# Layer 1's totals over channels and keys: 32x32 transpositions, VectorE sums and one small product each, in place of products with a matrix of ones

## The chip, the cores and the metric

The kernel runs on one core of one Trainium2 chip. The metric is the device time of one launch in microseconds. The core has five engines with instruction streams of their own: PE (TensorE, matrix products; its weight loads are listed apart as PEld), DVE (VectorE), ACT (ScalarE), POOL (GpSimd) and SP (SyncE, which here only issues DMAs). They wait for each other through semaphores. Everything is float32.

## The reference, cut to what matters

Two layers are computed on x of shape (8, 512, 32, 32), that is 8 images of C = 512 channels and N = 1024 positions. Layer 0 is an attention with group norms and 8 heads and is not touched by the change. Layer 1 is this, with one head of 512 channels:

```python
w_qkv = _weight_norm(v_qkv, g_qkv)
qkv = jnp.einsum('oc,bcn->bon', w_qkv, xt)
rms = jnp.sqrt(jnp.mean(jnp.square(qkv), axis=1, keepdims=True)) + 0.0001
qkv = qkv / rms
scores = jnp.einsum('bci,bcj->bij', q, k) * C ** (-0.5)
attn = jax.nn.softmax(scores, axis=-1)
h = jnp.einsum('bij,bcj->bci', attn, v)
h = jnp.einsum('oc,bcn->bon', w_out, h)
return (x + h) * 2.0 ** (-0.5)
```

Two totals over rows of a matrix matter here. The mean of squares (`rms`) needs, for each of the 1024 positions, a total over channels. The softmax needs, for each of the 1024 queries, a total of exponentials over the 1024 keys. In the kernel channels and keys both lie on the 128 partitions, so both totals run across partitions.

## The kernel before

One image is one *block* (`b`, 0 to 7); a block takes some 392 us. The program order on every engine is the order in which the Python code issues the instructions (`InOrder`, lines 26 to 34), so the order in the text is the order in each queue. A block has two parts.

**The heads of layer 0** (`Heads`, lines 534 to 628) run 32 steps: scores on PE, maxima and 32x32 transpositions on DVE, exponentials on ACT, scaling on POOL, and DMAs that regroup the transposed probabilities. Projections for the next block are woven in.

**Layer 0's end and layer 1.** `finish_layer0` (line 813) projects and normalises; then `Layer1.project` (line 895) does the following.

- Lines 900 to 908: four products with a Gram matrix (`py`), each multiplied with x on DVE and added to `acc`, a 128x1024 tile. Summed over partitions, `acc` is the square sum of each position. `acc` and `part` are the two halves of the tile `xy`.
- Lines 1014 to 1018: two `score_unit`s. Each is a `Seven` (lines 722 to 811): seven products `p_u`, of two matmuls with 512 columns each, where a plain product would take eight, drained by DVE and ACT into `u`. Inside the first unit, behind its third product (`(m, k) == (0, 2)`), `square_sums` (line 916) runs: eight products `ss`, with 128 columns of `acc` as the weights each, and two columns of ones. DVE turns `ss` into `rinv` = 1/rms with 14 small operations (`rsqrt` is three Newton steps). `broadcast` (line 925) writes `rinv` to DRAM (`far_rinv`, element by element, as the partition is the inner index there) and reads it back as a row on all partitions (`rrow`, in the place of `part`). POOL multiplies `u` by `rrow`.
- Lines 1023 to 1026: four `value_unit`s (`p_v`); ACT scales half of their results by `rinv`.
- Lines 1034 to 1037: four `weight_unit`s (`p_e`). ACT takes exponentials into `e`, and POOL adds them up into two 128x512 tiles `esum`, one for each half `th` of the queries (lines 1006 to 1009). In the last unit the half `th` = 1 is finished first.

Then the block's last loop (lines 1327 to 1340) runs the products `po` = v times e for `th` = 0, and the four groups of channels `c`, each of eight matmuls into one PSUM bank. `total(th)` (line 1042) multiplies `esum` with a matrix that is filled with the square root of 2 (`pe`, 512 columns; the result is the total, repeated on all partitions) and takes the reciprocal of it on DVE. `keep(th, c)` (line 1057) multiplies `po` by it and adds to x. The loads of x for block b + 2 (`load_x`, line 1325) are issued ahead of the loop; their statistics follow at `c` = 2 (lines 1331 to 1335), and the group norm's small products `pm` and `pv` at `norm_step`: `pm` in the middle of `c` = 3, `pv` in the middle of the product behind the loop (line 1343). Then the next block's heads start with `scores(0)` (line 1347). The products `th` = 1, `c` = 1 to 3 are done between the next heads' first steps (line 1348). For the last block they stand alone (lines 1356 to 1359).

PSUM comes from two pools. `ps_s` has three tiles of two banks (`wide`, tag `sc`), used in turn by the `Seven`s' products, `py`, `pe`, the norm's `pm` and `pv`, and the heads' scores. `ps_m` has two tiles of one bank (`bank`, tag `mm`). A tile can be taken anew only when all that read its predecessor in the same place are done.

Of the kernel before, what the change touches and what calls it, by code (L numbers as in the profile page):

```python
# [8 lines left out]
F32 = mybir.dt.float32  # L9
I32 = mybir.dt.int32  # L10
AF = mybir.ActivationFunctionType
ALU = mybir.AluOpType
AX = mybir.AxisListType
P = 128
# [38 lines left out]
def attention_blocks_kernel(  # L53
# [41 lines left out]
    pair = ctx.enter_context(tc.tile_pool(name="pair", bufs=2))  # L95
    prob = ctx.enter_context(tc.tile_pool(name="prob", bufs=2))
    block = ctx.enter_context(tc.tile_pool(name="block", bufs=2))
    sum_pool = ctx.enter_context(tc.tile_pool(name="sums", bufs=2))
    small = ctx.enter_context(tc.tile_pool(name="small", bufs=3))
    dram = ctx.enter_context(tc.tile_pool(name="dram", bufs=1, space=DRAM))  # L100
    ps_s = ctx.enter_context(tc.tile_pool(name="ps_s", bufs=3, space=PSUM))
    ps_m = ctx.enter_context(tc.tile_pool(name="ps_m", bufs=2, space=PSUM))
# [75 lines left out]
    for g in range(NG):  # L178
        VE.tensor_scalar(gavg[:, g, :], gavg[:, g, :], member[:, g : g + 1], None, ALU.mult)
    gavg = gavg.rearrange("p g s -> p (g s)")  # L180
    ones = const.tile([P, P], F32, name="ones")
    VE.memset(ones, 1.0)
    root2 = const.tile([P, P], F32, name="root2")
    VE.memset(root2, 2.0 ** 0.5)
    shift = const.tile([P, 1], F32, name="shift")
    VE.memset(shift, -16.0)
    cols = const.tile([P, NCOLS], F32, name="cols")
# [6 lines left out]

    def rsqrt_steps(r, v, n, name):

        t = small.tile([P, 4 * CI], F32, tag="rs_t", name=f"rs_{name}")[:, :n]
        VE.tensor_scalar(r.bitcast(I32), v.bitcast(I32), -0.5, 1597463007.0, ALU.mult, ALU.add)
        yield
        for _ in range(3):  # L200
            VE.scalar_tensor_tensor(t, r, -0.5, r, ALU.mult, ALU.mult)
            VE.tensor_mul(t, t, v)
            VE.scalar_tensor_tensor(r, t, 1.5, r, ALU.add, ALU.mult)
            yield
# [19 lines left out]
    far["qk0"] = dram.tile([P, 2, CI, P], F32, tag="far_qk0", name="far_qk0")  # L224
    far["qk7"] = dram.tile([P, 14, C - P], F32, tag="far_qk7", name="far_qk7")
    near = {}
    far_rinv = dram.tile([NT, P], F32, tag="far_rinv", name="far_rinv")

    def place(name, b):
        tag, shape = places[name]  # L230
# [87 lines left out]
    class Norm1:  # L318


        def __init__(self, b, xt, bank=bank):
            self.b, self.xt = b, xt
            self.st = small.tile([P, CI, 2, 6], F32, tag="gn_st1", name=f"st1_{b}")
            self.mv = small.tile([P, CI, 2], F32, tag="gn_mv1", name=f"mv1_{b}")
            self.gn = GroupNorm(self.mv, CI, G1S, G1B, f"1_{b}", bank)

# [327 lines left out]
    def finish_last(b, h, xt, o, begun):  # L654

        def project_out(j, th, pm):
            terms = out_terms(h.a, j, th, range(CI // 2, CI))
            if j in begun.pm:  # L660
                PE.matmul(pm[:, th, :], *terms[1], start=False, stop=True)
            else:
                run(matmuls(pm[:, th, :], terms))

        st = small.tile([P, CI, 2, 6], F32, tag="gn_st2", name=f"st2_{b}")
        mv = small.tile([P, CI, 2], F32, tag="gn_mv2", name=f"mv2_{b}")
        for j in range(CI):
            pm = begun.pm[j] if j in begun.pm else wide(f"pp_{b}_{j}")
            for th in range(2):
                project_out(j, th, pm)  # L670
            VE.tensor_add(o[:, j, :], o[:, j, :], pm.rearrange("p a f -> p (a f)"))
            for k in range(2):
                gn_stats(st[:, j], o[:, j, :], k)
            VE.bn_aggr(mv[:, j, :], st[:, j])
        fetch("gram", b)
        norm = GroupNorm(mv, CI, G2S, G2B, f"2_{b}")
        norm.means()
        a, c = norm.coeffs()
        for j in range(CI):
            AC.activation(o[:, j, :], o[:, j, :], AF.Identity, bias=c[:, j : j + 1], scale=a[:, j : j + 1])  # L680
            VE.tensor_add(xt[:, j, :], xt[:, j, :], o[:, j, :])
        slots.give(f"a_{b}")
        slots.give(f"o_{b}")
# [129 lines left out]
    def finish_layer0(b, h, rhs, xt, v0):  # L813

        o, w = big(f"o_{b}"), near["proj7"]
        st = small.tile([P, CI, 2, 6], F32, tag="gn_st2", name=f"st2_{b}")
        mv = small.tile([P, CI, 2], F32, tag="gn_mv2", name=f"mv2_{b}")
        norm = GroupNorm(mv, CI, G2S, G2B, f"2_{b}")

# [64 lines left out]
    class Layer1:  # L884
# [4 lines left out]
        def __init__(self, b, xt):  # L889
            self.b, self.xt = b, xt  # L890
            self.rhs = RightSide(xt, *(block.tile([P, 2, 2, HN], F32, tag="pb", name=f"t{k}_{b}") for k in (12, 34)))
            self.right = self.rhs.columns
            self.e, self.sums = {}, {}

        def project(self, hn_next):
            b, xt = self.b, self.xt
# [10 lines left out]
                if cj:  # L907
                    VE.tensor_add(acc, acc, part)

            ss = ps_m.tile([P, NT, 2], F32, tag="mm", name=f"ss_{b}")  # L910
            rinv = self.rinv = small.tile([P, NT], F32, tag="rinv", name=f"rinv_{b}")
            ms = small.tile([P, NT], F32, tag="ms", name=f"ms_{b}")
            rrow = part
            waiting = []

            def square_sums():
                for t in range(NT):
                    PE.matmul(ss[:, t, :], acc[:, t * P : (t + 1) * P], ones[:, :2], start=True, stop=True)
                VE.tensor_scalar(ms, ss[:, :, 0], 1.0 / (3 * C), 0.0, ALU.mult, ALU.max)
                rsqrt(rinv, ms, NT, f"r_{b}")  # L920
                VE.tensor_mul(rinv, rinv, ms)
                VE.tensor_scalar_add(rinv, rinv, 1e-4)
                VE.reciprocal(rinv, rinv)

            def broadcast():

                SY.dma_start(out=far_rinv.rearrange("t p -> p t"), in_=rinv)
                SY.dma_start(out=rrow, in_=far_rinv.rearrange("t p -> (t p)").partition_broadcast(P))
                for f in waiting:
                    f()  # L930
                waiting.clear()
                self.rrow = rrow
# [40 lines left out]
            def sum_u():  # L973

                s12 = prob.tile([P, 2, 2, HN], F32, tag="p", name=f"s12_{b}")
                s34 = prob.tile([P, 2, 2, HN], F32, tag="p", name=f"s34_{b}")
                q1, q2 = halves_
                self.s12, self.s34 = s12, s34
                for th in range(2):
                    e[th] = big(f"e_{b}_{th}", NT)  # L980
                    self.sums[th] = sum_pool.tile([P, HN], F32, tag="esum", name=f"esum_{b}_{th}")
                VE.tensor_add(s12[:, 0], u[:, :2, q2], u[:, 2:, q2])
                yield
                VE.tensor_sub(s12[:, 1], s12[:, 0], u[:, :2, q1])
                yield
                VE.tensor_sub(s34[:, 0], u[:, :2, q1], u[:, :2, q2])
                yield
                VE.tensor_sub(s34[:, 1], u[:, 2:, q1], s12[:, 1])

            def weight_unit(m):  # L990
# [9 lines left out]

                def last(which):
                    th, t = int(which[0]) - 1, m + 4 * (int(which[1]) - 1)
                    et, esum = c[which], self.sums[th]
                    AC.activation(et, et, AF.Exp, bias=shift, scale=rinv[:, t : t + 1])
                    done[th].append(et)
                    if len(done[th]) == 2:
# [6 lines left out]
            done = ([], [])  # L1013
            for m in range(2):
                for k, _ in enumerate(score_unit(m).steps()):
                    if (m, k) == (0, 2):
                        square_sums()
                        broadcast()
            if b + 1 < B:
                for j in (1, 2):  # L1020
# [18 lines left out]
            Seven.half = None  # L1039
            slots.give(f"u_{b}")  # L1040

        def total(self, th):

            pe = ps_s.tile([P, HN], F32, tag="sc", name=f"pe_{self.b}_{th}")
            PE.matmul(pe, root2, self.sums[th], start=True, stop=True)
            VE.reciprocal(self.sums[th], pe)

        def products(self, th, c, between=None):
            self.po = bank(f"po1_{self.b}_{th}_{c}")
            e = self.e[th]  # L1050

            terms = [(self.v[:, t, c * P : (c + 1) * P], e[:, t, :]) for t in (0, 4, 1, 5, 2, 6, 7, 3)]
            for k, _ in enumerate(matmuls(self.po, terms)):
                if k == 1 and between:
                    between()

        def keep(self, th, c):

            hs = slice(th * HN, (th + 1) * HN)

            share = near["v#"][:, N : N + HN] if self.b + 1 < B else self.po
            VE.tensor_mul(share, self.po, self.sums[th])
            VE.scalar_tensor_tensor(self.xt[:, c, hs], self.xt[:, c, hs], 2.0 ** -0.5, share, ALU.mult, ALU.add)
            if th == 1:
                SY.dma_start(out=ov[self.b, :, c, :], in_=self.xt[:, c, :])
# [136 lines left out]
    for b in range(B):  # L1202
# [117 lines left out]
        if b + 2 < B:  # L1320

            hn_next = big(f"hn_{b + 2}")
            norm1 = Norm1(b + 2, hn_next, lambda name: wide(name)[:, 0])
            for c in range(CI):
                load_x(b + 2, hn_next, c)
            steps = norm1.gn.all_steps()
        for c in range(CI):
            one.products(0, c, norm_step if c == CI - 1 else None)
            if c == 0:
                one.total(0)  # L1330
            if c == 2 and b + 2 < B:
                for ci in range(CI):
                    for k in range(2):
                        norm1.stats(ci, k)
                norm1.aggregate()
            if c == CI - 1:
                norm_step()
            one.keep(0, c)
            if c == 1:
                one.total(1)  # L1340
        slots.give(f"e_{b}_0")
        if more:
            one.products(1, 0, norm_step)
# [49 lines left out]
```

## Time and profile before

| what | value |
|---|---|
| time, median of 3 runs | 3246.95 us (3246.25 to 3247.75) |
| the profiled execution's own time | 3249.17 us |
| its span in the trace | 3246.7 us |
| granted TensorE clock, mean | 0.998 of full speed |
| DVE busy | 2274.4 us, 70% |
| POOL busy | 1253.0 us, 39% |
| reciprocal of `pe`, 128x512 | 16 times, mean 3353 ns |
| `ss` matmuls in the records | 128 (two records for one float32 product), busy 14.7 us |
| `pe` matmuls in the records | 32, busy 16.3 us |
| write of `rinv` to DRAM, 4 KB | 10.7 us from issue to landing |
| read of it to all partitions, 512 KB | 5.2 us |

The span runs from the first to the last instruction in the trace. "Busy" is the time in which an engine has at least one instruction in work; ends of matmuls are modelled, so a busy PE need not be at its peak. The chain of waits is followed back from the last instruction: at each step to whatever released it, or to the instruction ahead of it on its engine.

### The profile page before, as it was taken

Reading aid. Unit: us, or ns where it says so; the run is one execution under the profiler, and the core shown is the slowest. Engines: PE = TensorE matmul, PEld = TensorE weight load, DVE = VectorE, ACT = ScalarE, POOL = GpSimd, SP = SyncE. Lnnn points to the kernel's source line nnn. Section 1 sums busy time; section 2 is a strip of 40 time slices with the busy share of each in tenths; the row PEclk is TensorE's granted clock in tenths of the full one; section 3 lists DMA queues with packets and bytes.
Section 4 is the critical chain, followed back from the end, with each engine's and each line's share of the span. In section 5 each row is a group of like instructions: output and inputs, shape, how many; then the busy total and the mean of one; then the engine's idle time right before and its main releaser. Section 6 shows DMA issues by size and latency. Waiting matters only on the chain.

```text
span 3246.7 us, 36723 instructions
## 1 busy us (share of the span) xinstructions
PE 3217.5 (99%) x13346; PEld 1657.8 (51%) x13346; DVE 2274.4 (70%) x3074; ACT 1045.7 (32%) x1813; POOL 1253.0 (39%) x1025
## 2 busy tenths in 40 slices
PE   8999999999999999999999999999999999999899
PEld 5445644455444554445544555445554456444454
DVE  5697667876678756886668866687667876578643
ACT  2453114521145211551215412254123531145210
POOL 1554224732257212671227603265223642246121
PEclk9999999999999999999999999999999999999999
DMA  6776215862168511784228822388214872158500
GB/s 201 213 203 209 75 49 155 219 193 59 49 183 229 171 43 56 202 229 138 52 77 214 229 96 63 95 219 242 78 49 115 216 214 75 23 157 210 183 7 26
DMA packets 231579, 447.34 MB, mean 138 GB/s; under 512 B 28996, under 2 KB 69480, under 8 KB 225512
## 3 DMA queue, kind: packets, MB, share of 16 engines
q1 hardware_dynamic: 231280, 444.97, 49.0%
q8 instruction: 107, 1.75, 0.2%
q14 instruction: 72, 0.59, 0.1%
q10 hardware_dynamic: 120, 0.02, 0.0%
HBM read 133.06 MB, written 29.52 MB: 50 GB/s over the span
## 4 chain that ended last, share of the span: by engine, by line
PE 93%; DMA 3%; DVE 2%; SPq 1%; issue 1%; POOL 0%; DVEq 0%
PE po L34 26%; PE s L34 13%; PE pq L34 7%; PE p_e_T L34 7%; PE p_v_T L34 6%; PE p_e_B L34 5%; PE p_v_B L34 5%; PE py L34 4%; PE pqk L34 4%; PE p_u_T L34 3%; PE p_o_T L34 3%; DMA pT<-pb 3%; PE p_u_B L34 3%; PE p_o_B L34 2%; SPq L34 1%; DVE pb L34 1%
## 5 line engine op out<-in xcount | busy, mean ns | idle before, releaser
L34 POOL TENSOR_SCALAR p<-p,tt 128x1024 f32<-128x1024 f32 x512 | 565.9, 1118 | 753.7 <-DVE tt L34 734.9
L34 ACT ACTIVATE p<-s,nm 128x1024 f32<-128x1024 f32 x512 | 565.7, 1109 | 887.7 <-DVE nm L34 794.1
L34 DVE TENSOR_REDUCE nm<-s 128x1 f32<-128x1024 f32 x512 | 602.0, 1217 | 158.9 <-PE s L34 158.6
L34 DVE STREAM_TRANSPOSE pb<-p 128x2048 f32<-128x2048 f32 x256 | 589.6, 2303 | 45.6 <-DMA pT<-pb 20.8
L34 PE MATMUL s<-qk 64*128 64x512 f32 x2048 | 526.5, 604 | 0.6
L34 PE MATMUL po<-pT,v 128*64 128x256 f32 x4096 | 471.7, 383 | 3.5 <-DMA pT<-pb 3.4
L34 PE MATMUL po<-e,v 128*128 128x512 f32 x1024 | 451.7, 595 | 0.0
L34 PEld LDWEIGHTS po<-pT,v 128*64 128x64 f32 x4096 | 285.9, 137 | 220.8 <-ACT v L34 32.6
L34 PEld LDWEIGHTS s<-qk 64*128 64x128 f32 x2048 | 199.5, 186 | 253.3 <-issue 227.9
L34 PEld LDWEIGHTS po<-e,v 128*128 128x128 f32 x1024 | 191.9, 190 | 245.0 <-issue 236.4
L34 POOL TENSOR_TENSOR u<-u,xy 128x512 f32<-128x512 f32 x64 | 78.9, 1270 | 335.4 <-DMA xy<-far_rinv 261.4
L34 PE MATMUL pq<-hn,qk 64*128 64x512 f32 x504 | 197.1, 592 | 0.0
L34 POOL TENSOR_TENSOR esum<-esum,e 128x512 f32<-128x512 f32 x96 | 130.5, 1360 | 154.2 <-ACT e L34 151.7
L34 POOL TENSOR_TENSOR x<-x,o 128x1024 f32<-128x1024 f32 x21 | 52.1, 2512 | 348.3 <-ACT o L34 348.3
L34 ACT ACTIVATE e<-e,shift,rinv 128x512 f32<-128x512 f32 x128 | 100.9, 812 | 256.6 <-DVE e L34 256.6
L34 DVE TENSOR_TENSOR e<-e,p_e_T 128x512 f32<-128x512 f32 x160 | 106.9, 684 | 86.5 <-PE p_e_T L34 84.3
L34 DVE TENSOR_TENSOR v<-v,p_v_T 128x256 f32<-128x256 f32 x300 | 114.2, 415 | 68.7 <-PE p_v_T L34 50.0
L34 PE MATMUL pqk<-hn,qk 64*128 64x512 f32 (+1 forms) x672 | 158.2, 590 | 0.0
L34 PE MATMUL pq<-t,qk 64*128 64x512 f32 x336 | 150.9, 589 | 0.0
L34 PE MATMUL pq<-v,qk 64*128 64x512 f32 x336 | 150.9, 589 | 0.0
L34 PE MATMUL p_e_T<-s,t 128*128 128x512 f32 x320 | 147.8, 592 | 0.0
L34 PE MATMUL py<-x,gram 128*128 128x512 f32 x320 | 140.2, 597 | 5.4 <-issue 5.4
(215 smaller groups left out, 4130.9 us busy)
## 6 DMA issues: line engine op xcount, KB each, us to landing
pT<-pb SPq DMA_DIRECT2D x1024, 256.0 KB, 4.4
qk<-far_qk SPq DMA_DIRECT2D x21, 896.0 KB, 8.6
hn<-in_x_dram SPq DMA_DIRECT2D x32, 512.0 KB, 5.8
x<-in_x_dram SPq DMA_DIRECT2D x32, 512.0 KB, 4.5
out_dram<-x SPq DMA_DIRECT2D x32, 512.0 KB, 3.8
score<-far_score SPq DMA_DIRECT2D x8, 1792.0 KB
value<-far_value SPq DMA_DIRECT2D x8, 1792.0 KB, 7.2
proj<-far_proj SPq DMA_DIRECT2D x7, 1792.0 KB
```

Source lines behind the costliest of these rows:

```text
L34: return lambda *args, **kw: self._pin(call(*args, **kw))
```

## The change

All weights of the products with ones become a matrix `same` that holds 1 where two partitions have the same number modulo 32, and all data are folded by 32 first. `VE.transpose` turns each 32x32 square of a tile, and `tensor_reduce` adds up each 32 neighbouring columns; both together leave, from 128x1024, a tile of 128x32 in which partition 32 g + j and column B hold the sum over the 32 partitions of group g for position 32 B + j. One product with `same` adds the four groups g and leaves the total on each of the four. From there a 32x32 transposition gives 32 rows of 32 positions; `spread` writes them to DRAM as one row and reads that row to all partitions.

For the square sums this takes the place of eight products, and `rinv` is taken out of the 32-column form by four small copies. The small product moves behind the fourth product of the first score unit. For the exponentials it takes the place of two products of 512 columns and of two reciprocals of 128x512; one reciprocal of 128x32 and the way through DRAM come in. Both halves of `esum` are one tile now. In the last loop `po` lies two by two in `wide` tiles, `keep` runs for two groups of channels at once behind each second one, the loads of x are split in two (two ahead of the loop, two behind the spread), and so are the statistics. Some small tiles move to a pool with one buffer.

```diff
     block = ctx.enter_context(tc.tile_pool(name="block", bufs=2))
-    sum_pool = ctx.enter_context(tc.tile_pool(name="sums", bufs=2))
+    sum_pool = ctx.enter_context(tc.tile_pool(name="sums", bufs=1))
     small = ctx.enter_context(tc.tile_pool(name="small", bufs=3))
+    tiny = ctx.enter_context(tc.tile_pool(name="tiny", bufs=1))
     dram = ctx.enter_context(tc.tile_pool(name="dram", bufs=1, space=DRAM))
...
     gavg = gavg.rearrange("p g s -> p (g s)")
-    ones = const.tile([P, P], F32, name="ones")
-    VE.memset(ones, 1.0)
-    root2 = const.tile([P, P], F32, name="root2")
-    VE.memset(root2, 2.0 ** 0.5)
+    SQ = 32
+    same = const.tile([P, P], F32, name="same")
+    same2 = const.tile([P, P], F32, name="same2")
+    VE.tensor_reduce(flat := tiny.tile([P, SQ], F32, tag="flat", name="member32"), ident.rearrange("p (g i) -> p i g", i=SQ), AX.X, ALU.add)
+    for g in range(P // SQ):
+        VE.tensor_copy(same[:, g * SQ : (g + 1) * SQ], flat)
+    VE.tensor_scalar_mul(same2, same, 2.0 ** 0.5)
     shift = const.tile([P, 1], F32, name="shift")
...
-        t = small.tile([P, 4 * CI], F32, tag="rs_t", name=f"rs_{name}")[:, :n]
+        t = tiny.tile([P, SQ], F32, tag="rs_t", name=f"rs_{name}")[:, :n]
         VE.tensor_scalar(r.bitcast(I32), v.bitcast(I32), -0.5, 1597463007.0, ALU.mult, ALU.add)
...
     near = {}
-    far_rinv = dram.tile([NT, P], F32, tag="far_rinv", name="far_rinv")
+    far_rows = {k: dram.tile([SQ, SQ], F32, tag=f"far_{k}", name=f"far_{k}") for k in ("rinv", "esum")}
+    def square_sums(part, src, turned):
+        VE.transpose(turned, src)
+        VE.tensor_reduce(part, turned.rearrange("p (B j) -> p B j", j=SQ), AX.X, ALU.add)
+    def spread(row, vals, k, name):
+        flat = tiny.tile([P, SQ], F32, tag="flat", name=f"flat_{name}")
+        VE.transpose(flat, vals)
+        SY.dma_start(out=far_rows[k], in_=flat[:SQ])
+        SY.dma_start(out=row, in_=far_rows[k].rearrange("B i -> (B i)").partition_broadcast(P))
...
             self.b, self.xt = b, xt
-            self.st = small.tile([P, CI, 2, 6], F32, tag="gn_st1", name=f"st1_{b}")
+            self.st = tiny.tile([P, CI, 2, 6], F32, tag="gn_st1", name=f"st1_{b}")
             self.mv = small.tile([P, CI, 2], F32, tag="gn_mv1", name=f"mv1_{b}")
...
-        st = small.tile([P, CI, 2, 6], F32, tag="gn_st2", name=f"st2_{b}")
+        st = tiny.tile([P, CI, 2, 6], F32, tag="gn_st2", name=f"st2_{b}")
         mv = small.tile([P, CI, 2], F32, tag="gn_mv2", name=f"mv2_{b}")
...
         o, w = big(f"o_{b}"), near["proj7"]
-        st = small.tile([P, CI, 2, 6], F32, tag="gn_st2", name=f"st2_{b}")
+        st = tiny.tile([P, CI, 2, 6], F32, tag="gn_st2", name=f"st2_{b}")
         mv = small.tile([P, CI, 2], F32, tag="gn_mv2", name=f"mv2_{b}")
...
             self.right = self.rhs.columns
-            self.e, self.sums = {}, {}
+            self.e, self.sums, self.po = {}, None, {}
...
-            ss = ps_m.tile([P, NT, 2], F32, tag="mm", name=f"ss_{b}")
+            part_ss, r32, ms = (tiny.tile([P, SQ], F32, tag=t, name=f"{t}_{b}") for t in ("part", "r32", "ms"))
             rinv = self.rinv = small.tile([P, NT], F32, tag="rinv", name=f"rinv_{b}")
-            ms = small.tile([P, NT], F32, tag="ms", name=f"ms_{b}")
             rrow = part
             waiting = []
-            def square_sums():
-                for t in range(NT):
-                    PE.matmul(ss[:, t, :], acc[:, t * P : (t + 1) * P], ones[:, :2], start=True, stop=True)
-                VE.tensor_scalar(ms, ss[:, :, 0], 1.0 / (3 * C), 0.0, ALU.mult, ALU.max)
-                rsqrt(rinv, ms, NT, f"r_{b}")
-                VE.tensor_mul(rinv, rinv, ms)
-                VE.tensor_scalar_add(rinv, rinv, 1e-4)
-                VE.reciprocal(rinv, rinv)
+            square_sums(part_ss, acc, part)
+            def roots():
+                ss = bank(f"ss_{b}", SQ)
+                PE.matmul(ss, same, part_ss, start=True, stop=True)
+                VE.tensor_scalar(ms, ss, 1.0 / (3 * C), 0.0, ALU.mult, ALU.max)
+                rsqrt(r32, ms, SQ, f"r_{b}")
+                VE.tensor_mul(r32, r32, ms)
+                VE.tensor_scalar_add(r32, r32, 1e-4)
+                VE.reciprocal(r32, r32)
 ...
-                SY.dma_start(out=far_rinv.rearrange("t p -> p t"), in_=rinv)
-                SY.dma_start(out=rrow, in_=far_rinv.rearrange("t p -> (t p)").partition_broadcast(P))
+                spread(rrow, r32, "rinv", f"r_{b}")
+                for g in range(P // SQ):
+                    gs = slice(g * SQ, (g + 1) * SQ)
+                    VE.tensor_copy(rinv[gs], r32[gs].rearrange("p (t g) -> p g t", g=P // SQ)[:, g])
                 for f in waiting:
...
                 self.s12, self.s34 = s12, s34
+                self.sums = sum_pool.tile([P, N], F32, tag="esum", name=f"esum_{b}")
                 for th in range(2):
                     e[th] = big(f"e_{b}_{th}", NT)
-                    self.sums[th] = sum_pool.tile([P, HN], F32, tag="esum", name=f"esum_{b}_{th}")
                 VE.tensor_add(s12[:, 0], u[:, :2, q2], u[:, 2:, q2])
...
                     th, t = int(which[0]) - 1, m + 4 * (int(which[1]) - 1)
-                    et, esum = c[which], self.sums[th]
+                    et, esum = c[which], self.sums[:, halves_[th]]
                     AC.activation(et, et, AF.Exp, bias=shift, scale=rinv[:, t : t + 1])
...
                 for k, _ in enumerate(score_unit(m).steps()):
-                    if (m, k) == (0, 2):
-                        square_sums()
+                    if (m, k) == (0, 3):
+                        roots()
                         broadcast()
...
-        def total(self, th):
-            pe = ps_s.tile([P, HN], F32, tag="sc", name=f"pe_{self.b}_{th}")
-            PE.matmul(pe, root2, self.sums[th], start=True, stop=True)
-            VE.reciprocal(self.sums[th], pe)
-        def products(self, th, c, between=None):
-            self.po = bank(f"po1_{self.b}_{th}_{c}")
+        def square_sums(self):
+            self.part = tiny.tile([P, SQ], F32, tag="part", name=f"part_e_{self.b}")
+            turned = prob.tile([P, N], F32, tag="p", name=f"turned_{self.b}")
+            for th in (1, 0):
+                hs, n = slice(th * HN, (th + 1) * HN), SQ // 2
+                square_sums(self.part[:, th * n : (th + 1) * n], self.sums[:, hs], turned[:, hs])
+        def total(self):
+            pe = ps_s.tile([P, SQ], F32, tag="sc", name=f"pe_{self.b}")
+            PE.matmul(pe, same2, self.part, start=True, stop=True)
+            inv = tiny.tile([P, SQ], F32, tag="r32", name=f"inv_e_{self.b}")
+            VE.reciprocal(inv, pe)
+            spread(self.sums, inv, "esum", f"e_{self.b}")
+        def products(self, th, c, between=None, po=None):
+            po = self.po[th, c] = bank(f"po1_{self.b}_{th}_{c}") if po is None else po
             e = self.e[th]
 ...
             terms = [(self.v[:, t, c * P : (c + 1) * P], e[:, t, :]) for t in (0, 4, 1, 5, 2, 6, 7, 3)]
-            for k, _ in enumerate(matmuls(self.po, terms)):
+            for k, _ in enumerate(matmuls(po, terms)):
                 if k == 1 and between:
...
-            share = near["v#"][:, N : N + HN] if self.b + 1 < B else self.po
-            VE.tensor_mul(share, self.po, self.sums[th])
+            po = self.po.pop((th, c))
+            share = near["v#"][:, N : N + HN] if self.b + 1 < B else po
+            VE.tensor_mul(share, po, self.sums[:, hs])
             VE.scalar_tensor_tensor(self.xt[:, c, hs], self.xt[:, c, hs], 2.0 ** -0.5, share, ALU.mult, ALU.add)
...
             norm1 = Norm1(b + 2, hn_next, lambda name: wide(name)[:, 0])
-            for c in range(CI):
+            for c in range(2):
                 load_x(b + 2, hn_next, c)
             steps = norm1.gn.all_steps()
+        one.square_sums()
         for c in range(CI):
-            one.products(0, c, norm_step if c == CI - 1 else None)
+            if c % 2 == 0:
+                po = wide(f"po1_{b}_0_{c}")
+            one.products(0, c, norm_step if c == CI - 1 else None, po[:, c % 2])
             if c == 0:
-                one.total(0)
-            if c == 2 and b + 2 < B:
-                for ci in range(CI):
+                one.total()
+                if b + 2 < B:
+                    for ci in range(2, CI):
+                        load_x(b + 2, hn_next, ci)
+            if c and b + 2 < B:
+                for ci in range(CI)[2 * c - 2 : 2 * c]:
                     for k in range(2):
                         norm1.stats(ci, k)
-                norm1.aggregate()
+                if c == 2:
+                    norm1.aggregate()
             if c == CI - 1:
                 norm_step()
-            one.keep(0, c)
-            if c == 1:
-                one.total(1)
+            if c % 2:
+                one.keep(0, c - 1)
+                one.keep(0, c)
         slots.give(f"e_{b}_0")
```

## The prediction

> **What bounds the kernel now.** I read the page first: the line of busy times, and the shares of the chain of waits.
>
> ```profile
> PE 3217.5 (99%) x13346; PEld 1657.8 (51%) x13346; DVE 2274.4 (70%) x3074; ACT 1045.7 (32%) x1813; POOL 1253.0 (39%) x1025
> PE 93%; DMA 3%; DVE 2%; SPq 1%; issue 1%; POOL 0%; DVEq 0%
> ```
>
> PE is busy 99% of the span. A busy PE could still be one that waits with its modelled ends drawn out, so next come the waits of PE: over the whole run 23 us, nearly all in the first 10 us and in the last block, and only 3.4 us of it in the heads:
>
> ```profile
> PE po L34 <- DMA pT<-pb: 3.4, 3, 2.8
> ```
>
> Then the chain in order of time, for the first block (start, duration; x counts records, two for each float32 product). The other blocks have the same distances within 0.1 us.
>
> ```profile
> 355.92 3.43 PE p_u_B L34 x8
> 359.36 1.72 PE p_u_T L34 x4
> 361.07 1.68 PE ss L34 x16
> 362.75 5.26 PE p_u_T L34 x12
> ...
> 453.98 6.87 PE po L34 x16
> 460.85 0.86 PE pe L34 x2
> 461.71 6.87 PE po L34 x16
> 468.57 0.86 PE pe L34 x2
> 469.43 10.30 PE po L34 x24
> 479.73 0.12 PE pm L34 x2
> 479.85 6.97 PE po L34 x16
> 486.82 0.12 PE pv L34 x2
> 486.94 3.54 PE po L34 x8
> 490.48 1.92 PE s L34 x8
> ```
>
> Each piece starts where the one before it ends. So in layer 1 PE's own instructions are the path, and what is taken off PE there moves all that follows.
>
> **The sum on PE.** From 359.36 to 368.01 stand 16 `p_u` records (6.87 at their pace) and `ss`: `ss` costs 8.65 - 6.87 = 1.78 us. Two `pe` cost 469.43 - 453.98 - 2 x 6.87 = 1.71. Gone: 3.49 us a block. New: two products with 128 columns of weights and 32 moving columns. Their nearest row is `pm` and `pv` (4 columns, the same weights): from 469.43 to 490.48 stand three groups of `po` (20.61) and these two, so 0.22 each, 0.44 together. Saved: 3.05 us a block, times 8 = **24.4 us**. Bounds of a small product: 0.12 (its own piece in the chain) and 0.4 (two weight loads of 190 ns fully exposed), so 26.0 to 21.5 in all.
>
> One rule speaks against this sum. The Trainium skill, "TensorE: Matmul & The Clock Gate", section "Back-to-back issue gap", gives 1 to 64 moving columns some 60 cycles, 25 ns. By that the 16 `ss` records cost 0.4 us, and the change saves only 1.7 + 0.4 - 0.1 = 2.0 us a block, 16 in all. The row has 1.68 / 16 = 105 ns a record, because weights change each time; the same page's "LDWEIGHTS" (128 columns / 1.2 = 107 ns) fits it. I take the row.
>
> **Square sums: is the new product ready?** DVE finishes `acc` at 358.45 (the last `xy<-xy` starts at 357.22 and takes 1.23). Then comes a transposition of 1024 columns (estimate 1.17, half of the heads' 2303 ns for 2048 plus a little) and a reduction of 1024 (1217 ns by the heads' maxima): ready at about 361.0. PE is there behind the fourth `p_u` product, at 355.92 + 4 x 1.72 = 362.8. It doesn't wait; the cover is 1.8 us. Behind the 2.4 us on DVE stand the first unit's drains: `u<-u,p_u_B` at 360.01 moves to 361. Their PSUM tile is needed again by the seventh product at 366.4, so that is covered by 5 us. The 14 small operations are at 0.20 us spacing for 8 columns and some 0.23 for 32; with the transposition and four copies (0.15 to 0.2 each) DVE is through at about 367.5, 2 us later than now. The drains of products 5 and 6 queue behind and end near 369.5; their tile is taken anew at 373.3. Nothing on PE. Were the cover gone, each us would cost 8.
>
> The row through DRAM: now the write is issued at 365.63 and the read at 374.78, landing at 380.0, as POOL's `u` shows.
>
> ```profile
> 365.63 0.38 SPq L34 DMA_DIRECT2D far_rinv<-rinv  x1
> 374.78 0.33 SPq L34 DMA_DIRECT2D xy<-far_rinv  x1
> ```
>
> The write took 9.15 us because it is 1024 pieces of 4 bytes (the DMA view of this window counts 1056 packets under 512 B). Now it is 32 pieces of 128 bytes: at least 2 us, at most 9.15. Nearest by kind is `out_dram<-x`, 512 KB to DRAM in 3.8; I take 3. So `rrow` comes around 375, 5 us earlier. `u` is needed only by the `sum_u` additions and `p_e` from 394 on, so that gains nothing. SP's next DMA (`qk<-far_qk`) waits for PE until 381.7, so no queue behind it is touched.
>
> **Exponentials.** Times from here count from the start of `po` (453.98 now). POOL's last `esum` addition ends at 4.3 (455.66 + 2.61). DVE's last `e` addition ends at 1.35. DVE does the half `th` = 1 first, under POOL's end, then transposition (0.6) and reduction (0.62) of `th` = 0: ready at 5.6. PE needs it after eight matmuls, at 6.87: cover 1.3 us. If the single `esum` tile made DVE's first half wait for POOL's last addition, it would be 6.8, and the cover nearly gone. The product ends at 7.1. Reciprocal of 32 columns: from 8 columns (202 ns) and 512 (3353 ns), 0.35 us; transposition 0.15: write issued at 7.7, read at 10.7, **landed at 15.9**. `keep(0,0)` and `keep(0,1)` want to start at 6.87 x 2 + 0.22 = 14.0: DVE stands 1.9 us longer, four operations of 0.72 end at 18.8. The two 3.35 us reciprocals are gone from it, so DVE has the time.
>
> What waits behind these keeps? (a) Their PSUM tile is `pm`'s, two tiles later. (b) The statistics of channels 2 and 3: four of 0.6, then the aggregation 0.41 (now 473.21 to 478.32 for all eight), so 21.6. Their x is issued behind the read, at about 11, and four such loads landed in 6.7 us at most in this stage (1.3 us each once they flow), so by 18. `pm` is due at 3 x 6.87 + 0.22 + 3.43 = 24.3. **Cover 2.7 us**, where before it was 1.4 (aggregated at 478.32, `pm` at 479.73). (c) `scores(0)` takes the tile of `po` 2 and 3: their keeps end near 31.5, and PE is there at 34.9.
>
> The second rule that speaks against the change: "DMA: Bandwidth & Descriptors", section "Anatomy of one DMA", puts a fixed 2.0 us on each transfer, and here two of them are laid in line where a 3.35 us reciprocal stood. With 436 GB/s it makes 2.0 + 3.2, landing at 12.9: never late. By today's rows for this very pair (9.15 + 5.2) it lands at 22.0; the aggregation is ready at 27.7, `pm` waits 3.5 us in the six blocks that have it (0 to 5), and 21 of the 24.4 us are lost. My value lies between, by the broadcast's own row.
>
> **At nothing:** the matrix `same`, some 0.8 us more on DVE, in the 1.04 us for which it waits ahead of `cols` at 4.3 us (up to 0.3 if it doesn't fit). The one-buffer tiles: `st`, `part`, `r32` and the scratch are written and read once a block, or by DVE alone in order. The single `esum`: its predecessor's last reader is in the next heads. The transpositions' `turned` tile takes the place of `s12`, last read by PE 3.5 us before the `po`. The last block's end: `po`, two DVE operations, one DMA, as before.
>
> **Rivals.**
>
> 1. *The saved time is lost later.* The heads start 3 us earlier and might wait there for something that doesn't move. For it: the chain goes through DMA, DVE and POOL from 529 to 564 in the first block. Against: PE waits only 3.4 us for it in all, and what that chain starts from (`scores(0)`) moves along. Half lost: 3246.95 - 12 = 3235.
> 2. *DVE's fold is late for the small products* (cover 1.8 and 1.3 us). At a delay of 1 us beyond the cover in one place: 8 us lost, 3231.
> 3. *Slower: the row through DRAM.* Place: `pm`, behind the statistics, behind the keeps, behind the read. It decides from a pair of DMAs above 8.2 + 2.7 = 10.9 us; gains are all gone when the pair takes 10.9 + 24.4 / 6 = 15.0, and at 17 the stall is 6.1 x 6 = 36.6: 3259. For it: today's pair takes 14.4. Against: its write is of 4-byte pieces, and a 512 KB write takes 3.8 here.
> 4. *It doesn't do what it says:* the small products cost as much as the old. Excluded by the `pm` row.
>
> **How the numbers follow.** The sum is made against the profiled execution: 3246.7 - 24.4 = 3222.3 of span; that execution took 3249.17, 2.2 over the runs' median, so I set the saving against the median: 3246.95 - 24.4 = **3222.5**. Chances: forecast (3220 to 3226) 0.72; rivals 1 and 2 together 0.15; the row through DRAM eating most of it, 3238 to 3250, 0.07; slower by it 0.06. Two in ten left out: 3218 to 3236. What a measurement can tell from no change is 0.2%, 6.5 us: faster 0.87, same 0.06, slower 0.07.
>
> **What would show it.** PE: `ss` and `pe` with two records a block each, 0.2 us; no PE wait in layer 1; each block 3.0 us shorter. DVE: `esum` reciprocal at 0.35 us. DMA: the new writes near 3 us, and `keep(0,0)` starting about 2 us after the second `po` group. A wait of `pm` on DVE `mv`, or of `ss` or `pe` on DVE `part`, would prove me wrong, as would PE waits in the heads.

## The result, and the profile after

The changed kernel takes **3224.07 us** (median of 4 runs, 3223.5 to 3226.86); the kernel before took 3247.35 us beside it (3246.25 to 3249.39). The ratio is **0.9924, 95% interval 0.9913 to 0.9936**: faster by 23.3 us where 24.4 were forecast. The profiled execution has a span of 3222.0 us, 24.7 less than the one before, at the same granted clock (0.998).

The busy times from the page of the changed kernel, then the two waits of PE in the heads, from its list of waits (total, times, longest, in us):

```profile
PE 3192.6 (99%) x13218; PEld 1645.9 (51%) x13218; DVE 2279.2 (71%) x3166; ACT 1045.5 (32%) x1813; POOL 1253.2 (39%) x1025
```

```profile
PE po L34 <- DMA pT<-pb: 3.0, 2, 2.6
PE s L34 <- POOL qk L34: 0.5, 1, 0.5
```

The second is not in the list of the kernel before; both together are 3.5 us, where the heads waited 3.4 before. PE is 24.9 us less busy and the span 24.7 us shorter; PE is still busy 99% of it. DVE is 4.8 us busier: it lost 53.6 us of large reciprocals and got transpositions and sums for them, and that cost nothing.

Now the chain of waits in order of time, first block (start, duration, records):

```profile
357.21 3.43 PE p_u_B L34 x8
360.65 3.43 PE p_u_T L34 x8
364.08 0.14 PE ss L34 x2
364.22 3.52 PE p_u_T L34 x8
...
453.71 6.87 PE po L34 x16
460.58 0.14 PE pe L34 x2
460.72 17.25 PE po L34 x40
477.97 0.12 PE pm L34 x2
...
488.71 1.92 PE s L34 x8
```

`ss` has 2 records where it had 16, `pe` 2 where there were 4 of 512 columns, and each piece still begins where the last ends. I compared the starts of PE's stages in the two traces, block by block. From `p_u` to `p_e` each block is 1.56 us shorter, from `p_e` to `po` the same to 0.01, from `po` to the next `s` 1.50 shorter:

| where | changed kernel, first trace | second trace |
|---|---|---|
| up to the first `py` | +1.3 us | +0.3 us |
| eight times layer 1 | -24.5 us | -24.5 us |
| the seven times heads between | -1.6 us | +0.4 us |
| in the last block, ahead of `p_u` | +0.1 us | +0.3 us |
| span | -24.7 us | -23.5 us |

So the gain is made in layer 1 and kept; the rest is about 1 us of scatter in either direction.

What follows speaks of *cover*: the time by which a result is ready before PE needs it. The *row* is the 1024 reciprocals of the exponentials' totals, read from DRAM to all partitions. Its way and what hangs on it is best read from VectorE's timeline of the changed kernel, same block (start, duration; in brackets the idle time before and what ended it):

```profile
458.78 0.69 DVE L34 TENSOR_REDUCE part_e<-turned 128x16 f32<-128x512 f32 x1
460.76 0.36 DVE L34 RECIPROCAL inv_e<-pe 128x32 f32<-128x32 f32 x1 [1.29 <-PE pe L34]
461.15 0.21 DVE L34 STREAM_TRANSPOSE flat_e<-inv_e 128x32 f32<-128x32 f32 x1
...
467.71 0.69 DVE L34 TENSOR_TENSOR v<-po,esum 128x512 f32<-128x512 f32 x1 [3.99 <-PE po L34]
...
472.88 0.41 DVE L34 BATCH_NORM_AGGREGATE mv<-st 128x2 f32<-128x12 f32 x4
478.12 0.16 DVE L34 TENSOR_TENSOR d<-mv,pm 128x4 f32<-128x4 f32 x1 [4.84 <-PE pm L34]
```

And the two DMAs from SP's timeline:

```profile
461.39 0.32 SPq L34 DMA_DIRECT2D far_esum<-flat_e  x1
462.79 0.33 SPq L34 DMA_DIRECT2D esum<-far_esum  x1
```

When the row lands in this block the trace doesn't say directly: a landing of this read is recorded for block 6 alone, 3.7 us behind the issue. Blocks 6 and 7 have no loads of x behind the read; blocks 0 to 5 have two, issued 0.4 us later. A run further down (one bank for each group of channels), in which VectorE waits for the row in every block, has 4.3 to 4.5 us from issue to use in blocks 0 to 5, and 3.7 to 3.8 in blocks 6 and 7. With 4.3 the row lands at about 467.1 here, an estimate. The first keep (467.71) is released by PE, so the row is some 0.6 us early. In block 3 it isn't: there the write took 1.92 us to the next issue, not 1.40, and the first keep waits for the row, in this trace and in the second one:

```profile
1635.72 0.69 DVE L34 TENSOR_TENSOR v<-po,esum 128x512 f32<-128x512 f32 x1 [4.32 <-DMA esum<-far_esum]
```

PE loses nothing by that. (The expectations for the runs with one bank each, the 4-byte write and the delayed row still count with block 6's 3.7 us in every block, so with a row that is 1.1 us early.) In the first block the aggregation ends at 473.3 and `pm` runs at 477.97, 4.7 us of cover; the row's own cover at `pm` is that and its 0.6, some 5.3 us.

### The profile page after: what moved, and what is told of

It is laid out like the page before. It is cut to its first block, busy times and chain, and to the rows that moved or that the text cites. A ratio compares the mean times of both kernels' runs of the same rounds, so it can differ in the third digit from the quotient of the medians.

```text
span 3222.0 us, 36603 instructions
## 1 busy us (share of the span) xinstructions
PE 3192.6 (99%) x13218; PEld 1645.9 (51%) x13218; DVE 2279.2 (71%) x3166; ACT 1045.5 (32%) x1813; POOL 1253.2 (39%) x1025
## 4 chain that ended last, share of the span: by engine, by line
PE 93%; DMA 3%; DVE 2%; SPq 1%; issue 1%; POOL 1%; DVEq 0%; ACTq 0%; POOLq 0%
PE po L34 26%; PE s L34 13%; PE pq L34 7%; PE p_e_T L34 7%; PE p_v_T L34 6%; PE p_e_B L34 5%; PE p_v_B L34 5%; PE pqk L34 4%; PE py L34 4%; PE p_u_T L34 3%; PE p_o_T L34 3%; PE p_u_B L34 3%; PE p_o_B L34 2%; DMA pT<-pb 2%; DVE pb L34 1%; PE pv L34 1%
```

## The experiments

Ratios are to the kernel before, run beside each; a difference to the changed kernel is taken between ratios, times 3250 us. The theory is that PE's own instructions in layer 1 are the path, so that the gain is what PE no longer does there, as long as three chains stay under cover: the fold of `acc`, the fold of `esum`, and the row through DRAM. The rivals: that the gain is VectorE's relief from the large reciprocals; that the new waits cost something after all.

### The two halves of the change alone, and the whole again

Only the square sums folded. The exponentials' part is as before, with the old last loop: one bank for each group of channels, all loads of x ahead of it.

```diff
...
-            PE.matmul(pe, same2, self.part, start=True, stop=True)
+            PE.matmul(pe, root2, self.sums[th], start=True, stop=True)
+            VE.reciprocal(self.sums[th], pe)
...
```

> Only the square sums go through the fold; the exponentials' totals stay as two products of 512 columns with two reciprocals of 128x512. My theory (what PE no longer does in layer 1 is the gain, block by block): 1.78 - 0.23 = 1.55 us a block, 12.4 us in all, 3247.4 - 12.4 = 3235, ratio 0.996. Rival (the gain comes from VectorE being relieved of the large reciprocals): VectorE only gets more to do here, so no gain or a loss, 3247 or more.

Measured: 3236.2 us, ratio 0.9959 (0.9946 to 0.9971).

Only the exponentials folded (the square sums as before, behind the third product):

```diff
...
-                PE.matmul(ss, same, part_ss, start=True, stop=True)
+                for t in range(NT):
+                    PE.matmul(ss[:, t, :], acc[:, t * P : (t + 1) * P], ones[:, :2], start=True, stop=True)
...
```

> Only the exponentials' totals go through the fold; the square sums stay as eight products with two columns of ones, behind the third product. My theory: 1.71 - 0.22 = 1.49 us a block, 11.9 us in all, 3235.4, ratio 0.996; with the run of the square sums alone it adds up to the whole. Rival (relief of VectorE): the whole 23 us, 3224.

Measured: 3233.05 us, ratio 0.9949 (0.9937 to 0.9962).

The changed kernel unaltered:

> The changed kernel as it is, once more, for a second trace. Expected: ratio 0.992 to 0.993; in the trace layer 1 of each block again 3.06 us shorter than before. The start (1.3 us longer in the first trace) and the heads (from 0.8 us shorter to 1.1 us longer) differ from the first trace's where they are scatter; where the change causes them they come back in the same blocks.

Measured: 3224.99 us, ratio 0.9923 (0.991 to 0.9937).

The halves save 13 and 17 us, the whole 25, and the intervals allow a plain sum. The traces are sharper: in the first run each block is 1.56 us shorter from `p_u` to `p_e` and unchanged from `po` to `s`; in the second it is unchanged in the first and 1.49 shorter in the second. That is 12.5 and 11.9 us, 24.4 together. The half that only loads VectorE gains as much as the half that relieves it, so relief isn't the cause. The second trace of the whole has the same 24.5 us in layer 1. Its heads differ: block by block against before they were -0.8, -0.8, -0.7, +0.8, +1.1, -0.5, -0.7 us in the first trace and -1.3, -0.8, -0.4, 0.0, +1.1, +0.5, +1.4 in the second. The sums lie around zero; whether single blocks have a small share of their own isn't settled by this (all are measured against one trace of before).

### VectorE given back its reciprocals

Two reciprocals of 128x512 that nobody reads, directly behind the row's DMAs:

```diff
...
             spread(self.sums, inv, "esum", f"e_{self.b}")
+            VE.reciprocal(self.turned[:, :HN], self.turned[:, HN:])
+            VE.reciprocal(self.turned[:, :HN], self.turned[:, HN:])
```

> As the changed kernel, with two reciprocals of 128x512 per block added on VectorE that nobody reads, directly behind the DMAs of the row, so that VectorE has as much of them as before the change. My theory: VectorE has room there (it idles 4 us ahead of the first keep, and pm has 4.7 us of cover), the statistics and keeps move by 2.7 us at most, PE does not wait: 3225. Rival (the relief of VectorE is part of the gain): 12 us or more come back, 3237 or more.

Measured: 3224.55 us, ratio 0.9923 (0.991 to 0.9937), the same as the changed kernel. With as much reciprocal time as before the change the whole gain is still there. VectorE's relief is worth nothing here.

### What a small product costs

```diff
-                PE.matmul(ss, same, part_ss, start=True, stop=True)
+                for _ in range(9):
+                    PE.matmul(ss, same, part_ss, start=True, stop=True)
...
```

and the same for `pe`.

> As the changed kernel, with each of the two small products issued nine times: 128 more of them in all, with the same weights loaded each time. By the trace's price of the old products with changing weights (two records of 105 ns): 27 us lost, 3252. By the 60 cycles of 25 ns for each of the two records: 6.4 us, 3231. By the price of a single one in the trace (0.14 its own piece, 0.22 with what follows): 18 to 28 us.

Measured: 3252.23 us, ratio 1.0006 (0.9997 to 1.0015): 27.0 us more than the changed kernel for 128 products, **0.21 us each**. The chain of that run, around both products:

```profile
363.62 1.93 PE ss L34 x18
...
461.91 1.93 PE pe L34 x18
```

18 records in 1.93 us are 107 ns a record, with 32 columns; before, with two columns, it was 105 ns. So the number of columns hardly matters at this size. The trace has one weight load for each record (144 of each in `ss`), also where the weights stay the same, which fits a price set by the loads; that it is the load and nothing else in a product is not shown apart. The 25 ns a record that the prediction weighed against it are excluded: they would have made 6.4 us. And the gain is used up: nine small products in each place cost what the old products cost.

### The cover of the square sums' fold

The small product behind the third product of the score unit instead of the fourth, then behind the second:

```diff
-                    if (m, k) == (0, 3):
+                    if (m, k) == (0, 2):
```

> As the changed kernel, but the square sums' small product stands behind the third product of the score unit, where the old ones stood, not behind the fourth. In the trace VectorE's fold is ready at 362.3 and PE behind the third product at 362.4: my theory (cover counted from the two ends) is no wait or at most 0.1 us a block, 3225. Rival (the fold has more cover than that, or the later place was bought for another reason): no difference either, so the next run decides.

Measured: 3229.19 us, ratio 0.9937 (0.9924 to 0.9949). In the trace a block is 1.33 us shorter than before from `p_u` to `p_e` where it was 1.56: 0.22 us lost a block, 1.8 in all. The chain has `ss` with 0.37 us where it had 0.14, and PE's weight load for it waits for `part` in all eight blocks: in the changed kernel the load starts some 0.4 us ahead of the product (363.5 and 363.9), here both start together. Of the 4.6 us between the ratios the remainder isn't explained; the intervals overlap.

```diff
-                    if (m, k) == (0, 3):
+                    if (m, k) == (0, 1):
```

> As the changed kernel, but the square sums' small product stands behind the second product of the score unit, where PE is at 360.65, 1.65 us ahead of the fold. My theory: a wait of 1.7 us in each of the eight blocks, 13 us, 3238; if a wait also slows TensorE's clock behind it, as the waits of pm did in the run with the 4-byte write, up to 2 us more a block, 3254. Rival (PE's stream takes up such a wait, since half of its weight loads are ahead): 3225.

Measured: 3240.22 us, ratio 0.9974 (0.9964 to 0.9985). PE's list of waits has a new first line (total, times, longest):

```profile
PE ss L34 <- DVE part L34: 13.4, 8, 1.7
```

The wait is 1.68 us in each block, as worked out from the two ends (1.65). PE doesn't take it up: each block loses 1.95 us, the wait and again a longer `ss` (0.41 us in the chain), 15.6 in all, and the ratios give 16.6. So the fold has 1.8 us of cover behind the fourth product, nearly none behind the third, and the place one product later is what keeps it off the path.

### The row through DRAM: pairs or one by one

```diff
-            if c % 2 == 0:
-                po = wide(f"po1_{b}_0_{c}")
-            one.products(0, c, norm_step if c == CI - 1 else None, po[:, c % 2])
+            one.products(0, c, norm_step if c == CI - 1 else None)
...
-            if c % 2:
-                one.keep(0, c - 1)
-                one.keep(0, c)
+            one.keep(0, c)
```

> As the changed kernel, but each group of channels has its own PSUM bank of the two as before, and its keep runs directly behind it. The third group then needs the first one's bank. My theory, with the trace's row landing 12.8 us behind the start of the products: the first keep reads the bank until 13.5, PE is there at 13.9, so no wait, 3224. With the row of my prediction (15.9) it would wait 2.6 us in all eight blocks, 3245. Rival (the pairs are needed as the row is never in time): 3232 or more.

Measured: 3229.27 us, ratio 0.9936 (0.9922 to 0.9949): some 4 us slower than the changed kernel. No forecast held: neither no wait at all, nor 2.6 us in every block, nor the rival's 3232 or more. Its chain passes through the row (first block), and PE's list of waits has it in six blocks:

```profile
463.23 4.28 DMA esum<-far_esum
467.51 0.02 issue
467.53 0.70 DVE v L34
468.23 0.04 issue
468.28 10.57 PE po L34 x24
```

```profile
PE po L34 <- DVE v L34: 2.3, 6, 1.1
```

`po` of the third group starts at 468.28 instead of 468.05 (461.18 + 6.87): a wait of some 0.2 us here. My forecast of no wait was made with 3.7 us for the read, and that is block 6's; here the first block's took 4.28. From `po` to `s` blocks 0 to 5 lose 3.9 us in all, 1.4 of it in block 3, where the write took longer; block 6, which has no loads of x behind the read, loses nothing. So the pairs are worth about 4 us: with one bank each the row is just late in the blocks that load x.

### The row through DRAM made late

First by the old kind of write, 1024 pieces of 4 bytes:

```diff
-            spread(self.sums, inv, "esum", f"e_{self.b}")
+            SY.dma_start(out=far_rows["esum"].rearrange("B i -> i B"), in_=inv[:SQ])
+            SY.dma_start(out=self.sums, in_=far_rows["esum"].rearrange("B i -> (B i)").partition_broadcast(P))
```

> As the changed kernel, but the reciprocals of the exponentials' totals are written to DRAM element by element (1024 pieces of 4 bytes, as the old kernel wrote rinv) and not as 32 rows. My theory (the row through DRAM is on no path until it is 5.8 us later than in the trace: it lands 1.1 us ahead of the first keep, and the aggregation ends 4.7 us ahead of pm): the write takes 9.15 us to the next issue where it took 1.4, so the row is 7.75 us later and pm waits some 2 us in blocks 0 to 5: 12 us lost, 3237. Rival (keeps and statistics have cover that I don't see, pm does not wait): 3225. Second rival (every us of the row's delay costs in all blocks): 8 x 6.6 = 53 us, 3278.

Measured: 3235.54 us, ratio 0.9954 (0.9942 to 0.9967): 10 us lost. From issue to the next issue the write takes 7.56 us in the first block where rows take 1.40. PE's list of waits:

```profile
PE pm L34 <- DVE mv L34: 10.4, 7, 4.0
```

One of the seven, 4.0 us, is the last block's and was there before. The other six are the ones of blocks 0 to 5, 6.4 us together. The place is the forecast one: `pm`, behind the statistics, behind the keeps, behind the row. The length fits the cover of 5.3 us better than the 5.8 of my expectation: in the first block the read is issued 14.99 us behind the start of `po`, where it was 9.08, so 5.9 us later, and PE waits 0.72.

Then by 13.4 us of VectorE's time ahead of the row's transposition:

```diff
+            VE.reciprocal(self.turned[:, :HN], self.turned[:, HN:])
+            VE.reciprocal(self.turned[:, :HN], self.turned[:, HN:])
+            VE.reciprocal(self.turned[:, :HN], self.turned[:, HN:])
+            VE.reciprocal(self.turned[:, :HN], self.turned[:, HN:])
             spread(self.sums, inv, "esum", f"e_{self.b}")
```

> As the changed kernel, with four reciprocals of 128x512 per block, read by nobody, ahead of the row's transposition: the row is 13.4 us later. My theory (cover 5.8 us at pm, in the six blocks that have it): 7.6 x 6 = 46 us lost, 3271, slower than before the change. With the cover of 2.7 us that the prediction gave it (from 8.2 us for the pair of DMAs), 64 us: 3289. Rival (waits also in blocks 6 and 7): 61 us, 3286, and the trace then shows PE waits there.

Measured: 3291.0 us, ratio 1.0126 (1.0112 to 1.014): slower than before the change, 66 us more than the changed kernel. The time agrees best with the forecast for a cover of 2.7 us, but the waits don't:

```profile
PE pm L34 <- DVE mv L34: 52.9, 7, 8.3
```

Without the last block's 4.0 that is 48.9 in six blocks, 8.2 us each. A cover of 5.3 us makes it 8.1; my 5.8, with block 6's landing in it, made 7.6. Blocks 6 and 7 don't wait, as forecast: from `po` to `s` block 6 is 1.49 us shorter than before, as it is without the delay. But blocks 0 to 5 lose 10.1 to 11.5 us each, 2 to 3 more than they wait. Where this comes from is in the windows of that run (columns: stretch and length, busy us of PE, PEld, DVE, ACT and POOL with their instructions, PE's granted clock, DMA share, GB/s):

```profile
470.00:478.00 8.00, 8.00 (x20) 3.29 (x18) 7.09 (x7) 0.00 (x0) 0.00 (x0) 1.00 0.10 26
478.00:486.00 8.00, 0.18 (x1) 0.00 (x0) 5.06 (x8) 0.00 (x0) 0.00 (x0) 0.81 0.54 173
486.00:490.00 4.00, 3.53 (x6) 1.86 (x7) 0.97 (x9) 0.00 (x0) 0.00 (x0) 0.53 0.00 0
490.00:494.00 4.00, 4.00 (x11) 1.74 (x10) 1.90 (x3) 0.00 (x0) 0.00 (x0) 1.00 0.00 0
```

PE's granted clock falls during the wait (0.81 on the mean of its stretch) and is 0.53 in the 4 us behind it. The 16 `po` records after `pm` take 8.37 us instead of 6.97, and `pm` itself 0.59 instead of 0.12: together 1.9 us, what the first block lost beyond its wait. My expectation had priced the waiting alone.

## Why the prediction was right

**The sum on PE** held term by term. `ss` and `pe` were put at 3.49 us a block, their successors at 0.22 each, the difference at 3.05; the traces show 3.06. A new product's own piece is 0.14, and from 357.21 to 367.74 stand 24 records of `p_u` (10.30 at their pace) and `ss`, so 0.23 with what follows. Between the row of 105 ns a record and the 25 ns of the Trainium skill ("TensorE: Matmul & The Clock Gate", "Back-to-back issue gap") the row was to be taken: issuing the products nine times gave 107 ns. The reason given for it, that the weights change each time, did not hold: the nine products have the same weights.

**The square sums' fold** was put at 2.55 us behind `acc` with a cover of 1.8 us; it took 2.53 (transposition 1.25, sum 1.22), and the two moved-up runs measured the cover from the other side.

**The exponentials' fold**: ready 5.6 us behind the start of `po`, cover 1.3; measured 5.8 (458.78 + 0.69 - 453.71) and 1.1. The single `esum` tile does not make the first half wait for POOL: its transposition starts at 454.98, the second half's at 458.04.

**The row through DRAM** was mis-sized, with no effect. I took 3 us for the write, from a 512 KB write, and 5.2 for the read, from the same read before the change; they took 1.4 and some 4.3 where x is loaded too, so the row came some 13.4 us behind the start of `po`, not 15.9. Two things that I had left out work the other way: the read is longer in the blocks with loads of x behind it (3.7 us without them), and the write takes about 2 us in block 3. The skill's rule for the pair ("DMA: Bandwidth & Descriptors", "Anatomy of one DMA": 2.0 + 3.2) gives 5.2 us; measured are 5.1 without the loads and 5.7 with them, by a write that is shorter and a read that is longer than its terms. The section is about DMAs that GpSimd issues, and these are SyncE's, so that the sum comes near is no confirmation. The consequence was on the safe side: a cover at `pm` of 4.7 us and not 2.7, and keeps that wait for PE alone in all blocks but one. That no run takes away the loads of x on their own leaves their part a reading of blocks 0 to 5 against 6 and 7. Why the read of `rinv` takes 5.2 us in the old kernel, with nothing behind it, stays open; the write of 4-byte pieces ahead of it is not enough, as the read behind such a write took 3.8 us in block 6 of the run with the 4-byte write.

**The rivals.** Time lost later: the heads' sum of -1.6 and +0.4 us excludes half of the gain. A late fold: no wait of `ss` or `pe` on `part` in the changed kernel. The slower case named the right place and the right order of chain, and both late runs found it there; its price, the waiting alone, was too low: at 13.4 us of delay the waits are 48.9 us and the loss 66, with the clock low behind each wait. In the prediction a pair of 15.0 us uses up the gain; that number wasn't measured.

**At nothing**: the matrix `same` ended at 4.0 us, and VectorE still idled 0.63 us ahead of `cols`; it was under the cover named. The start was 1.3 us later in the first trace and 0.3 in the second; `pcol_g` waits for a DMA in both kernels, and the rest of it is not explained.

The runs point to no version that is better than the changed kernel. What is left of the two products is 16 x 0.22 = 3.5 us, half of what a measurement of this kernel can tell from no change.

## What to carry to other kernels

Where PE is the path, as here, a product with ones costs its records (105 ns each with two columns) or its columns (0.86 us with 512), not what it adds up: fold on an engine with room first, then one narrow product does. Count the cover of every chain that takes the old one's place from both ends, in a block where everything that shares the queue is under way, and place the product where the cover is more than the chain's own scatter. A way through DRAM goes off the path if the reader is put late enough and the write is in rows.

## What the runs showed that I had not expected

**A wait of PE can cost more than its length, and its length alone does not tell when.** In the run with the 4-byte write, five of the waits are short (0.72 us in the first block) and cost about 1.0 to 1.3 us each. In block 3 the row was later, and PE waited 2.18 us. Its PE timeline, and the windows over it:

```profile
1650.34 0.39 PE L34 MATMUL pm<-mv,gavg 128*128 128x4 f32 x2 [2.18 <-DVE mv L34]
1650.58 8.81 PE L34 MATMUL po<-e,v 128*128 128x512 f32 x16
```

```profile
1648.00:1652.00 4.00, 1.82 (x5) 0.94 (x5) 2.84 (x12) 0.00 (x0) 0.00 (x0) 0.84 0.00 0
1652.00:1656.00 4.00, 4.00 (x8) 1.70 (x7) 0.00 (x1) 0.00 (x0) 0.00 (x0) 0.73 0.02 4
1656.00:1660.00 4.00, 4.00 (x12) 1.86 (x11) 3.15 (x7) 0.00 (x0) 0.00 (x0) 1.00 0.00 0
```

The granted clock falls to 0.84 and 0.73, and the 16 records of `po` take 8.81 us instead of 7.11 in the first block. That block lost 4.1 us by a wait of 2.18. The eight waits of 1.68 us in the run behind the second product left the clock at 1.00 and lost 1.95 each. That looks like a step between 1.7 and 2.2 us, but other waits on record speak against one. In the last block's heads `po` waits for the same DMA in every run; here are the runs with the product nine times and with it behind the third, each with a window behind the wait:

```profile
3034.47 5.21 PE L34 MATMUL po<-pT,v 128*64 128x256 f32 x32 [2.36 <-DMA pT<-pb]
3036.00:3040.00 4.00, 4.00 (x28) 2.46 (x26) 1.82 (x1) 0.28 (x1) 0.00 (x0) 0.80 0.80 219
```

```profile
3015.74 3.67 PE L34 MATMUL po<-pT,v 128*64 128x256 f32 x32 [2.40 <-DMA pT<-pb]
3016.00:3020.00 4.00, 4.00 (x34) 2.81 (x31) 2.31 (x1) 0.47 (x1) 0.68 (x1) 1.00 0.86 206
```

Waits of 2.36 and 2.40 us, and only behind the first the clock was low (32 records in 5.21 us, not 3.67). In the records of the granted clock every low stretch, apart from one at the end of each run, lasts 3.41 us or two, three or four times that. So when a wait falls may count beside how long it is; no run tests it. The Trainium skill ("TensorE: Matmul & The Clock Gate", "Why this matters for your kernels") names gaps above some 3 us; here 2.18 and 2.36 us were enough, once each.

**A write of 4-byte pieces is slow, but not in moving its bytes.** In the old kernel the write of `rinv` is issued at 365.63 and the read at 374.78. The windows between (the last two columns are the DMA share and GB/s) show data moving in the first 2 us or so only:

```profile
366.00:368.00 2.00, 2.00 (x6) 0.91 (x5) 0.84 (x2) 0.00 (x0) 0.00 (x0) 1.00 0.23 2
368.00:374.80 6.80, 6.80 (x18) 2.97 (x17) 2.66 (x4) 0.58 (x1) 0.00 (x0) 1.00 0.00 0
```

What takes the other nearly 7 us isn't shown; the same 4 KB in 32 rows were through in 1.4 us altogether.
